# Background streams beside the first FFN of a macaron block: other places for transposes, routing and operand fetches

## The chip, the cores and the metric

The kernel runs on one core of a Trainium2 chip. The metric is the device time of one launch in microseconds, as the median of several runs. A core has five engines with an instruction queue each: TensorE (PE, matrix products into PSUM), VectorE (DVE), ScalarE (ACT), GpSimd (POOL) and SyncE (SP), which in this kernel issues the DMA transfers. Each engine takes its instructions in the order of the program, and engines wait for each other through semaphores.

## The reference, cut to what matters

The input x is (4, 1024, 128): 4096 tokens of width 128. A first mixture-of-experts FFN, an attention and a second FFN are added to it in turn:

```python
x = x + 0.5 * ffn(layernorm(x))
x = x + attn(layernorm(x))       # attn normalises its input again, adds it back
x = x + 0.5 * ffn(layernorm(x))

def ffn(x):                      # 8 experts, all of them computed for each token
    w = routing_weights(x, Wr, temperature)                # (.., 8)
    h = silu(einsum('btd,edi->beti', x, Wg)) * einsum('btd,edi->beti', x, Wu)
    return einsum('bte,betd->btd', w, einsum('beti,eid->betd', h, Wd))

def routing_weights(x, Wr, temperature):
    inh = sigmoid(x @ Wr / temperature)
    in_zone = (inh >= LOWER) & (inh <= UPPER)
    dist = abs(inh - 1 / e)
    w = exp(-dist / 0.1) * in_zone
    fb = exp(-dist / 0.3) * (one of its two largest)
    w = where(w.sum(-1) < 1e-8, fb / clip(fb.sum(-1), 1e-8), w)
    return w / clip(w.sum(-1), 1e-8)

def attn(x):                     # 16 heads of 64
    h = layernorm(x) * ln_scale + ln_bias
    c_q, c_kv = h @ w_down_q.T, h @ w_down_kv.T            # latents of width 64
    q, k = rope(c_q @ w_up_q.T), rope(c_kv @ w_up_k.T)
    v = c_kv @ w_up_v.T
    return softmax(q @ k.T / 8) @ v @ w_out.T + x
```

## The kernel before, in words

All 4096 tokens lie in SBUF as X, in eight blocks of 512 tokens. The kernel has three stages: the first FFN (about 10 to 231 us of the profile), the attention (about 235 to 1604 us) and the second FFN (to the end).

**The first FFN** (`ffn`) runs 64 iterations, n = 8 * block + expert. An iteration has six matmuls for the gate and the up product (L402, each product in three parts of a split into high and low halves), the silu on ACT (L404), the down product of the expert three iterations back (L373), the product of silu and up on DVE (L410), and the addition of a weighted expert output to X (`gather`): on DVE, or by a scaled copy on ACT (L385) and a sum on POOL (L386).

**Streams.** Between these, at four points of each iteration, `bg1` advances two generators that hold everything else. A generator does one step per `next` and pauses at each `yield`. A rate says how many steps a point is worth, with fractions saved up, so the place of each background instruction in each engine's queue follows from the counts of steps.

- Stream 0 (`RATE0` per point while n < 4, then `RATE1` = 2.4 steps an iteration) prepares the blocks in pairs (0,1), (2,3), (4,5), (6,7) with `ffn_pre`: statistics, the power on POOL, the norm (L225 on DVE for block 0, L227 on ACT for the others), four transposes on PE (L256) with copies on DVE (L258, L259), the router product (L269) with its reduction (L270), and for the pair together the routing (`route`). The number k is the step at which a part is done; the second block of a pair runs 5 steps behind the first. The first twelve steps of the first pair come before the FFN. The pairs (4,5) and (6,7) join the stream at n = 14.
- Stream 2 (`RATE2` = 2.3 steps an iteration until n = 46, `RATE3` = 1.4 after) holds the weights of the attention and from n = 16 `attn_first`: the attention's preparation of the first 1024 tokens (`attn_pre`: transposes L540, down products L546, transposes L561) and then nine rotations.

**Spare bank.** In the first FFN the transposes, router products and down products of the streams share one PSUM bank, `self.rest = [self.psS[3]]`, which `aux` hands out.

**Rotations** (`rope`). The 64 rotations make the rotated q and k, 512 tokens and two heads' worth at a time. One rotation fetches its operand C_l (two buffers, 512 KB) from DRAM ("fetch"), multiplies it (L595, "mm"), multiplies by cosines and sines on DVE (L583), adds on POOL (L602, L604), splits the result in halves (L609 on ACT, L613 on POOL) and stores both (hi_r and eo, "dhi" and "dlo"). `attn_first` starts a new rotation each 6 steps, and its table says how many steps before or after its "mm" each part is issued. Rotations 0 to 8 (`NROPE` = 9) belong to `attn_first`; what is left of them when the first FFN ends is issued there. Later ones follow the attention's loop.

**The seam.** At n = 46 `load(0)` brings q and k of the first heads in; from n = 49 on the attention's first pass for the row maxima (`passA`: L676 on PE, L677 on DVE) runs in the FFN already. After the FFN come `load(1)`, the rest of `attn_first`, and the fetch of rotation 9 (`rope(-1, {-2: "fetch"})`), all on SP's queue. Then the attention's loop: scores (L701), exponentials on ACT (L705), sums on POOL (L717), and values (L724).

**In `route`**, `more` is a further pause at four places. It was given by `self.slot >= 0`, and `self.slot` is negative until the attention begins:

```python
more = (None,) if self.slot >= 0 else ()
...
v.tensor_tensor(w, w, ge, ALU.mult)
yield from more
```

The last pair of the second FFN, (6,7), is prepared within it by `ffn_pre` too (`bg2`: one step an iteration from n = 17, two from n = 22).

Of the kernel before, what the change touches and what calls it, by code (L numbers as in the profile page):

```python
# [31 lines left out]
NROPE = 9  # L32
ACTS = (4, 6, 7)
WLAG, GS, GD = 4, 17, 22
RATE0, RATE1, RATE2, RATE3 = 1.55, 2.4, 2.3, 1.4


class Kernel:
# [191 lines left out]
    def ffn_pre(self, P, blks, xs, w_out, done=None, rows=None):  # L230
        nc = self.nc
        X = self.X
        n = len(blks)
        mv = P.tile([128, TPB, 2], F32, name="mvf")
        rstd = P.tile([128, TPB, 2], F32, name="rstdf")
        z = P.tile([128, TPB, E], F32, name="z")
        st = {}

        def stage(k, h, blk):
            t0 = 4 * blk  # L240
            hs = slice(4 * h, 4 * h + 4)
            src = [X[:, t0 + i, :] for i in range(4)]
            if k == 0:
                st["st", h] = self.small.tile([128, 4, 6], F32, name="st")
            if k in (0, 1):
                self.stats(st["st", h], src, mv[:, hs], rstd[:, hs], k)
            elif k == 3:
                self.power(rstd[:, hs])
            elif k in (5, 6):
                if k == 5:  # L250
                    st["y", h] = P.tile([128, 4, 128], F32, name="yf", tag="f0")
                self.norm(st["y", h], src, mv[:, hs], rstd[:, hs], k - 5, blk == 0 and done is None)
            elif k == 8:
                ps = self.aux()
                for i in range(4):
                    nc.tensor.transpose(ps[:, i * 128:(i + 1) * 128], st["y", h][:, i, :], self.ident)  # L256
                x2 = st["x", h] = xs(blk)
                nc.vector.tensor_copy(x2[:, 0, :], ps)  # L258
                nc.vector.tensor_tensor(x2[:, 1, :], ps, self.f(x2[:, 0, :]), ALU.subtract)  # L259
                self.ready.add(blk)  # L260
            elif k == 12:
                x2 = st["x", h]
                if done:
                    done(blk, x2)
                pz = self.aux()
                for i in range(4):
                    c = slice(i * 128, (i + 1) * 128)
                    for hl in range(2):
                        nc.tensor.matmul(pz[:, i * 16:(i + 1) * 16], x2[:, hl, c], self.wr[:, hl, :], start=hl == 0, stop=hl == 1)  # L269
                nc.vector.tensor_reduce(z[:, hs, :], pz[:, 0:64].rearrange("p (t k e) -> p t e k", t=4, k=2), AX.X, ALU.add)  # L270

        for k in range(14 + 5 * (n - 1)):
            yield any(k - 5 * h in (8, 12) for h in range(n))
            for h, blk in enumerate(blks):
                stage(k - 5 * h, h, blk)
        yield from self.route(P, 4 * n, z, w_out)
        if rows is not None:
            yield from self.weight_rows(P, rows)
        self.routed.update(blks)

    def route(self, P, T, z, w_out):

        nc = self.nc
        v, act, pool = nc.vector, nc.scalar.activation, nc.gpsimd
        sh, sh4 = [128, T, E], [128, T, E, E]
        bc = lambda t: t.unsqueeze(2).to_broadcast(sh)
        new = lambda name, shape, tag=None: P.tile([128, TPB] + shape, F32, name=name, tag=tag or name)[:, :T]


        inh, dist = new("inh", [E]), new("dist", [E])  # L290
        more = (None,) if self.slot >= 0 else ()
        yield
        act(inh, z[:, :T], AF.Tanh, scale=self.rtemp)
        act(inh, inh, AF.Identity, scale=0.5, bias=self.consts[:, 0:1])
        act(dist, inh, AF.Abs, bias=self.consts[:, 1:2])
        yield
        ex = P.tile([128, 2, TPB, E], F32, name="ex")[:, :, :T]
        dx = P.tile([128, 2, TPB, E], F32, name="dx")[:, :, :T]
        w, fb = ex[:, 0], ex[:, 1]
        act(w, dist, AF.Tanh, scale=-0.5 / 0.1)  # L300
        act(fb, dist, AF.Tanh, scale=-0.5 / 0.3)
        act(dx, ex, AF.Identity, scale=-1.0, bias=self.consts[:, 2:3])
        act(ex, ex, AF.Identity, bias=self.consts[:, 2:3])
        ge, le = new("ge", [E]), new("le", [E])
        pool.tensor_scalar(ge, inh, LOWER, None, ALU.is_ge)
        pool.tensor_scalar(le, inh, UPPER, None, ALU.is_le)
        pool.tensor_tensor(ge, ge, le, ALU.mult)
        yield
        v.reciprocal(dx, dx)
        yield  # L310
        pool.tensor_tensor(ex, ex, dx, ALU.mult)


        below = new("below", [E, E], "f1")
        pool.tensor_tensor(below, fb.unsqueeze(3).to_broadcast(sh4), self.tri.unsqueeze(1).to_broadcast(sh4), ALU.mult)
        yield
        v.tensor_tensor(w, w, ge, ALU.mult)
        yield from more
        s, ne, some = new("ws", []), new("ne", []), new("some", [])
        v.tensor_reduce(s, w, AX.X, ALU.add)  # L320
        v.tensor_scalar(ne, s, 1e-8, None, ALU.is_lt)
        v.tensor_scalar(some, s, 1e-8, None, ALU.is_ge)
        yield
        g = new("g", [E, E], "f0")
        v.tensor_tensor(g, fb.unsqueeze(2).to_broadcast(sh4), below, ALU.is_gt)
        yield
        v.tensor_reduce(le, g, AX.X, ALU.add)
        yield

        v.scalar_tensor_tensor(fb, le, 2.0, fb, ALU.is_lt, ALU.mult)  # L330
        yield from more
        r = new("fr", [])
        v.tensor_reduce(r, fb, AX.X, ALU.add)
        v.tensor_scalar(r, r, 1e-8, None, ALU.max)
        yield
        v.reciprocal(r, r)
        v.tensor_tensor(r, r, ne, ALU.mult)
        yield from more
        v.tensor_tensor(w, w, bc(some), ALU.mult)
        yield from more  # L340
        v.tensor_tensor(fb, fb, bc(r), ALU.mult)
        yield
        v.tensor_tensor(w, w, fb, ALU.add)
        v.tensor_reduce(s, w, AX.X, ALU.add)
        yield
        v.tensor_scalar(s, s, 1e-8, 2.0, ALU.max, ALU.mult)
        v.reciprocal(s, s)
        v.tensor_tensor(w_out, w, bc(s), ALU.mult)
# [270 lines left out]
    def attn_first(self):  # L619

        yield from self.attn_pre(0)
        steps = {-5: "fetch", 0: "mm e0 e1", 2: "e", 3: "o", 5: "hi0", 6: "hi1", 7: "dhi", 8: "lo", 10: "dlo"}
        for t in range(-5, 6 * (NROPE - 1) + 11):
            yield
            for n in range(NROPE):
                for stage in steps.get(t - 6 * n, "").split():
                    self.rope(n, stage)
# [146 lines left out]
    def run(self):  # L774
# [21 lines left out]
        with ExitStack() as ctx:  # L796
# [8 lines left out]
            wgen = self.ffn_weights1(fw, fp)  # L805
            first = pre(0, 0, 1)
            next(wgen)
            for n in range(12):
                next(first)
                if n in (5, 6):  # L810
                    next(wgen)
            self.router_weights()
            attn_weights = self.attn_weights()
# [47 lines left out]

        a, c, e = (NP - 3) % 3, (NP - 2) % 3, (NP - 1) % 3
        xs = [self.KT[c], self.QT[e], self.KT[e]]
        self.load(1)
        for _ in streams[2].pop() if streams[2] else ():
            pass
# [30 lines left out]
        def rope(g, table):  # L897
            for d, stages in table.items():
                n, r = divmod(g - d - 1, 4)
                if r == 0 and 0 <= n + NROPE < 16 * B and n >= 0:  # L900
                    for stage in stages.split():
                        self.rope(n + NROPE, stage)

        rope(-1, {-2: "fetch"})
        for g in range(NGRP + 1):
            s0 = 2 * g
            self.group, self.slot = g, s0
# [29 lines left out]
            if g < NGRP and g % 8 == 7:  # L937
                P = g // 8
# [91 lines left out]
```

## Time and profile before

| what | us |
|---|---|
| median of 3 runs (lowest, highest) | 1762.56 (1762.29, 1762.91) |
| the profiled execution's own time | 1766.25 |
| its span in the profile | 1764.5 |
| PE busy | 1681.8 |
| DVE, ACT, POOL busy | 1298.0, 912.9, 1463.0 |
| mean granted clock of PE | 0.986 |

The span runs from the first to the last instruction that the profile shows; the execution's own time has 1.75 us around it. Busy times are sums over an engine's instructions. A line of PE's timeline gives the start and the duration of a group of instructions, the engine, the line of the kernel, the output and the inputs, and in brackets the idle time before it and what ended that. A "granted clock" below 1 in a stretch means that PE ran below full speed there.

### The profile page before, as it was taken

To read this page: it belongs to the slowest core of one execution; us is meant where nothing else is said; L and a number is where in the kernel's file an instruction comes from. 1 tells how busy PE (TensorE), PEld (TensorE's weight loads), DVE (VectorE), ACT (ScalarE), POOL (GpSimd) and SP (SyncE) were. 2 spreads that over 40 slices of the span, in tenths; PEclk is the share of its full clock that TensorE was granted. 3 is DMA by queue.
4 is the path that set the end of the run, shared out by engine and by line. 5 is a ranking of instruction groups with operands and counts; after the bars stand their busy time and mean duration, and the time that the engine had idled before them with its cause. 6 is when DMAs were issued, how large, how long until landed. Compare 5 with 4: busy or idle time off the path is not lost.

```text
span 1764.5 us, 31143 instructions
## 1 busy us (share of the span) xinstructions
PE 1681.8 (95%) x11428; PEld 1009.1 (57%) x11428; DVE 1298.0 (74%) x2223; ACT 912.9 (52%) x1916; POOL 1463.0 (83%) x803
## 2 busy tenths in 40 slices
PE   6998989999999999999999999999999999999998
PEld 5777755555555555455555555555555555456777
DVE  6676757767877778877787777688677766835887
ACT  4666546455455444555544455444554544455554
POOL 4448779999899998999998899898999987676666
PEclk9999989999999999999999999999999999999999
DMA  6024445455445554445454544544455432024542
GB/s 201 1 72 160 151 132 144 133 151 149 111 126 140 142 135 121 121 133 144 133 133 121 145 130 124 145 120 121 121 145 142 121 99 62 1 86 114 138 127 101
DMA packets 241416, 215.99 MB, mean 122 GB/s; under 512 B 156784, under 2 KB 169712, under 8 KB 240624
## 3 DMA queue, kind: packets, MB, share of 16 engines
q1 hardware_dynamic: 241264, 214.01, 43.9%
q8 instruction: 89, 1.46, 0.4%
q14 instruction: 63, 0.52, 0.1%
HBM read 129.93 MB, written 84.02 MB: 121 GB/s over the span
## 4 chain that ended last, share of the span: by engine, by line
PE 76%; DVE 10%; ACT 6%; POOL 4%; issue 3%; DMA 1%; SPq 0%; ACTq 0%; POOLq 0%; DVEq 0%
PE psc L724 24%; PE ps_s L701 21%; PE ps_a L676 8%; ACT p L705 4%; PE ps_s L402 4%; PE ps_s L736 3%; PE ps_s L481 3%; DVE m L677 3%; PE psx L761 3%; POOL acc L717 2%; PE psx L436 2%; PE psx L595 2%; PE psc L373 1%; PE psc L481 1%; PE ps_s L546 1%
## 5 line engine op out<-in xcount | busy, mean ns | idle before, releaser
L677 DVE TENSOR_REDUCE m<-ps_a 128x2 f32<-128x1024 f32 x512 | 626.8, 1224 | 329.1 <-PE ps_a L676 328.1
L705 ACT ACTIVATE p<-ps_s 128x512 f32<-128x512 f32 x1024 | 530.3, 602 | 578.3 <-PE ps_s L701 549.5
L717 POOL TENSOR_TENSOR acc<-acc,p 128x1024 f32<-128x1024 f32 x320 | 762.1, 2382 | 60.0 <-ACT p L705 42.8
L724 PE MATMUL psc<-p,ckn 128*64 128x512 f32 x2048 | 498.9, 608 | 0.0
L701 PE MATMUL ps_s<-QT,KT 64*128 64x512 f32 x3072 | 446.4, 393 | 9.4 <-ACT dsb L738 6.1
L701 PEld LDWEIGHTS ps_s<-QT,KT 64*128 64x128 f32 x3072 | 290.8, 185 | 75.9 <-ACT dsb L738 9.2
L724 PEld LDWEIGHTS psc<-p,ckn 128*64 128x64 f32 x2048 | 124.7, 136 | 227.3 <-issue 216.0
L676 PE MATMUL ps_a<-KT,QT 64*128 64x512 f32 x1024 | 234.0, 450 | 18.8 <-DVE m L677 18.8
L676 PEld LDWEIGHTS ps_a<-KT,QT 64*128 64x128 f32 x1024 | 97.5, 184 | 239.9 <-DVE m L677 78.7
L717 POOL TENSOR_TENSOR acc<-p 128x1024 f32<-128x1024 f32 x64 | 151.7, 2371 | 67.4 <-ACT p L705 67.2
L701 PE MATMUL ps_s<-maxr,one_row 64*128 64x512 f32 x1024 | 206.3, 392 | 0.0
L613 POOL TENSOR_TENSOR eo<-eo,hi_r 128x1024 fp32r<-128x1024 f32 x64 | 154.0, 2407 | 19.3 <-ACT hi_r L609 19.3
L386 POOL TENSOR_TENSOR X<-X,dtmp 128x512 f32<-128x512 f32 x54 | 69.3, 1284 | 68.1 <-ACT dtmp L385 60.1
L701 PEld LDWEIGHTS ps_s<-maxr,one_row 64*128 64x128 f32 x1024 | 99.6, 185 | 21.8
L489 POOL TENSOR_TENSOR p<-eo,p 128x512 fp32r<-128x512 f32 x42 | 63.1, 1510 | 40.0 <-ACT p L488 34.9
L602 POOL TENSOR_TENSOR eo<-rt,rt 128x512 f32<-128x512 f32 x64 | 83.0, 1296 | 0.0
L766 DVE SCALAR_TENSOR_TENSOR X<-ps_s,rT,X 128x128 f32<-128x128 f32 x252 | 70.4, 341 | 16.7 <-PE ps_s L761 16.6
L604 POOL TENSOR_TENSOR eo<-rt,rt 128x512 f32<-128x512 f32 x64 | 82.4, 1287 | 0.0
L402 PE MATMUL ps_s<-xs,wg 128*128 128x512 f32 x192 | 66.3, 455 | 11.3 <-DVE p L410 10.1
L609 ACT CAST hi_r<-eo 128x512 fp32r<-128x512 f32 x128 | 74.0, 622 | 4.7 <-POOL eo L604 2.2
L766 DVE SCALAR_TENSOR_TENSOR X<-psx,rT,X 128x128 f32<-128x128 f32 x252 | 70.4, 342 | 0.0
L761 PEld LDWEIGHTS psx<-G,osb 64*128 64x128 f32 x504 | 65.5, 187 | 4.3
(190 smaller groups left out, 2197.7 us busy)
## 6 DMA issues: line engine op xcount, KB each, us to landing
C_l<-cs SPq DMA_DIRECT2D x64, 512.0 KB
QT<-qs SPq DMA_DIRECT2D x256, 128.0 KB
KT<-ks SPq DMA_DIRECT2D x256, 128.0 KB
qs<-hi_r SPq DMA_DIRECT2D x32, 512.0 KB
qs<-eo SPq DMA_DIRECT2D x32, 512.0 KB
ks<-hi_r SPq DMA_DIRECT2D x32, 512.0 KB
ks<-eo SPq DMA_DIRECT2D x32, 512.0 KB
wb<-wt SPq DMA_DIRECT2D x64, 256.0 KB
```

The lines of the kernel that those rows point to most:

```text
L402: nc.tensor.matmul(p, w[:, a, e, :], xs[:, c, :], start=k == 0, stop=k == 2)
L602: nc.gpsimd.tensor_tensor(w["eo"][:, 0, :], w[0, 0], w[1, 1], ALU.subtract)
L604: nc.gpsimd.tensor_tensor(w["eo"][:, 1, :], w[0, 1], w[1, 0], ALU.add)
L613: nc.gpsimd.tensor_tensor(w["eo"].bitcast(F32R), w["eo"], self.f(w["hi"]), ALU.subtract)
L676: nc.tensor.matmul(self.psA[:, hh, :], self.QT[P % 3][r, 0, q0:q0 + 128], self.KT[P % 3][r, 0, kk * 512:kk * 512 + 512], start=True, stop= ...
L677: nc.vector.tensor_reduce(self.m_of[U][:, :, qb, kk], self.psA, AX.X, ALU.max)
L701: nc.tensor.matmul(ps, w, x, start=k == 0, stop=k == 3)
L705: nc.scalar.activation(self.p_of[s][:, hh, :], ps, AF.Exp, scale=0.125)
L717: nc.gpsimd.tensor_tensor(acc, self.p_of[s - 1] if c == 1 else acc, self.p_of[s], ALU.add)
L724: nc.tensor.matmul(self.psC[64 * hh:64 * hh + 64, :], self.ckn[b % 2][:, c, :], self.p_of[s][:, hh, :], start=c == 0, stop=c == 7)
L761: nc.tensor.matmul(po[hh][:, i * 128:(i + 1) * 128], osb[r, i * 128:(i + 1) * 128], self.G[r, j, :], start=True, stop=True)
L766: nc.vector.scalar_tensor_tensor(x, po[hh][:, i * 128:(i + 1) * 128], rT[:, 4 * hh + i:4 * hh + i + 1], x, ALU.mult, ALU.add)
```

## The change

Four things are altered. In `ffn_pre` the transposes come at step 10 instead of 8 and the router product at step 14 instead of 12, for every pair; in the first FFN the second block of the first pair runs 9 steps behind the first instead of 5, and the first fourteen steps (twelve before) come ahead of the FFN. In `route` the four further pauses are also taken by the pairs (2,3), (4,5), (6,7) of the first FFN. The rotations of `attn_first` fetch their operand 8 steps before their product instead of 5, and `RATE2` is 2.4 instead of 2.3. The fetch of rotation 9 is issued directly after the first FFN, ahead of `load(1)`.

```diff
-RATE0, RATE1, RATE2, RATE3 = 1.55, 2.4, 2.3, 1.4
+RATE0, RATE1, RATE2, RATE3 = 1.55, 2.4, 2.4, 1.4
...
-            elif k == 8:
+            elif k == 10:
                 ps = self.aux()
...
-            elif k == 12:
+            elif k == 14:
                 x2 = st["x", h]
...
-        for k in range(14 + 5 * (n - 1)):
-            yield any(k - 5 * h in (8, 12) for h in range(n))
+        lag = 9 if blks[0] == 0 and done is None else 5
+        for k in range(16 + lag * (n - 1)):
+            yield any(k - lag * h in (10, 14) for h in range(n))
             for h, blk in enumerate(blks):
-                stage(k - 5 * h, h, blk)
-        yield from self.route(P, 4 * n, z, w_out)
+                stage(k - lag * h, h, blk)
+        yield from self.route(P, 4 * n, z, w_out, blks[0] > 0 or done is not None)
...
-    def route(self, P, T, z, w_out):
+    def route(self, P, T, z, w_out, late):
...
-        more = (None,) if self.slot >= 0 else ()
+        more = (None,) if late else ()
...
-        steps = {-5: "fetch", 0: "mm e0 e1", 2: "e", 3: "o", 5: "hi0", 6: "hi1", 7: "dhi", 8: "lo", 10: "dlo"}
-        for t in range(-5, 6 * (NROPE - 1) + 11):
+        steps = {-8: "fetch", 0: "mm e0 e1", 2: "e", 3: "o", 5: "hi0", 6: "hi1", 7: "dhi", 8: "lo", 10: "dlo"}
+        for t in range(-8, 6 * (NROPE - 1) + 11):
...
-            for n in range(12):
+            for n in range(14):
                 next(first)
-                if n in (5, 6):
+                if n in (5, 7):
                     next(wgen)
...
+        self.rope(NROPE, "fetch")
         self.load(1)
...
-        rope(-1, {-2: "fetch"})
```

## The prediction

> **What bounds the kernel now.** I read the page's totals and slices first, then what TensorE (PE) waited for in the first 240 us, then each such gap in the timeline with the queue it waited for, last the granted clock in stretches of 3.4 us.
>
> ```profile
> PE 1681.8 (95%) x11428; PEld 1009.1 (57%) x11428; DVE 1298.0 (74%) x2223; ACT 912.9 (52%) x1916; POOL 1463.0 (83%) x803
> PE   6998989999999999999999999999999999999998
> POOL 4448779999899998999998899898999987676666
> PEclk9999989999999999999999999999999999999999
> ```
>
> PE is the bound: 95% busy, its few dips in the first six slices (44 us each). The attention after them can give little: what is to be had is PE's gaps in the first FFN, up to 231 us, at the seam to the attention, and at the end. The waits name them (total, times, longest):
>
> ```profile
> PE ps_s L402 <- DVE p L410: 10.1, 7, 3.9
> PE ps_s L256 <- DVE yf L225: 7.0, 3, 6.6
> PE ps_s L402 <- ACT p L404: 4.1, 3, 2.6
> PE ps_s L256 <- ACT yf L227: 1.8, 3, 0.8
> PE psx L595 <- DMA C_l<-cs: 1.4, 1, 1.4
> ```
>
> Each kind has its place in PE's timeline:
>
> ```profile
> 75.64 0.71 PE L256 MATMUL ps_s<-ident,yf 128*128 128x128 f32 x2 [0.75 <-ACT yf L227]
> 104.95 1.65 PE L402 MATMUL ps_s<-xs,wu 128*128 128x512 f32 x3 [2.56 <-ACT p L404]
> 152.73 1.65 PE L402 MATMUL ps_s<-xs,wg 128*128 128x512 f32 x3 [3.92 <-DVE p L410]
> 187.15 0.49 PE L595 MATMUL psx<-C_l,wup 64*128 64x512 f32 x1 [1.42 <-DMA C_l<-cs]
> 245.74 0.79 PE L595 MATMUL psx<-C_l,wup 64*128 64x512 f32 x1 [3.46 <-DMA C_l<-cs]
> ```
>
> The 3.92 us at 152.73 go back to the last routing: DVE stood at L317 behind POOL, with L583 and L410 behind it. The 3.46 us at 245.74 go back to SP's queue, where the fetch of rotation 9 stood behind a store that waited for POOL:
>
> ```profile
> 148.44 0.23 DVE L317 TENSOR_TENSOR ex<-ex,ge 128x64 f32<-128x64 f32 x1 [3.55 <-POOL ex L311]
> ...
> 241.00 0.38 SPq L47 DMA_DIRECT2D qs<-eo  x1
> 241.43 0.47 SPq L47 DMA_DIRECT2D C_l<-cs  x1
> ```
>
> A gap also costs afterwards (window, length, PE busy, granted clock):
>
> ```profile
> 73.80:77.20 3.40, 1.77 (x12) 0.99 0.00 0
> 77.20:80.60 3.40, 3.40 (x9) 0.51 0.03 7
> 148.80:152.20 3.40, 0.01 (x1) 1.00 0.77 254
> 152.20:155.60 3.40, 2.87 (x7) 0.50 0.40 154
> ```
>
> The window after a half-empty one ran at half clock, and so gave away about 1.7 us. Eight such windows lie between 30 and 252 us.
>
> **Clock, row against rule.** The Trainium skill, "TensorE: Matmul & The Clock Gate", section "HAM oscillation — how this bites in real kernels", says: "The abstract rule is "no PE-idle gaps >~3.4µs."" By it only the gaps of 3.92 and 3.46 us carry a surcharge. The trace disagrees: 1.77 us of work in 3.40 (52%) was already followed by 0.51. By the rule the gaps of 75 to 110 us are worth their 6.9 us, by the trace 11.6. The measurement decides; but new short gaps then cost double too.
>
> **The change part by part**, against the profiled execution: span 1764.5, own time 1766.25 (1.75 around the span; 3.7 us or 0.2% above the median of 1762.56). I take the differences over to the median unchanged.
>
> 1. *Opening, n = 0 to 8* (first pair's second block 9 steps behind the first, all transposes and routers two steps later). Following the three queues by hand, the first L402 starts about 0.6 us earlier, that of n = 2 one later, n = 4 at 25.5 (26.76), n = 6 at 35.1 (34.46). DVE's norm (L225), copies and routing bound this stage, and none of it goes away. The first pair's routing still ends just ahead of the first gather. Value 0, bounds -1.5 and +1.5.
>
> 2. *Routing of blocks 2, 3* now at n = 13 to 18 with four more pauses. PE's gaps of 0.40 (62.19) and 0.44 (70.00) may go: -0.8 (-0.84 to 0).
>
> 3. *n = 18 to 30.* Before, blocks 4, 5 and the attention's first preparation both began at n = 16; now the blocks come some three iterations later. PE idled 0.75 + 0.82 + 1.28 + 0.27 + 0.39 + 2.56 + 0.87 = 6.9 us there, and three half-clock windows (77.2, 87.4, 104.3) cost 1.6 + 1.7 + 1.4 = 4.7: together 11.6. In the new order the two streams take turns on the single spare PSUM bank (L256, L269, L540, L546, L561). PE meets four places where a use follows another so closely that it waits for the reader of the first: I put 0.9 + 2.2 + 1.7 + 0.6 = 5.4 us on them, from the readers' rows (L258 0.68 and L259 0.69 on DVE, L562 0.42) and what is queued ahead of them (L410 0.63 to 0.68, L404). Nearest rows: waits of 0.62, 0.39 and 0.87 at such places before, and 98.39 to 102.84 (4.4 us) from an L546 to the L553 that read its result. Two half-clock windows with that: 3.3. So -11.6 + 8.7 = -2.9 (-8 to +4).
>
> 4. *n = 33 to 49*, routing of blocks 6, 7, now at n = 43 to 48. DVE's new order puts four L583 between L309 and L317, so POOL has some 3.8 us for L311, against the 3.55 us that DVE stood before. Gaps here: 0.50 + 3.92 + 0.23 + 1.03 = 5.7, half clock 1.4, together 7.1. But POOL was busy 40.49 us of the 46.70 from 128.60 to 175.30, and a rotation's sums (L602, L604, L613) are 1.29 + 1.28 + 2.38 = 4.97: when PE runs faster, POOL's ring of buffers is next. I credit a third: -2.5 (-5 to +2).
>
>    *Ports, row against rule.* "SBUF — State Buffer", section "Who interferes with whom", says that a DVE operation with two SBUF inputs and a GpSimd operation lock each other out for a whole instruction. That speaks against spreading a routing among a busy POOL: some 8 such operations, each held by up to one 1.28 us POOL operation, are 10 us of DVE. The trace shows less: L321 took 672 ns where its shortest took 171, and the last routing lost about 3.2 us in all that way. Its DVE was busy 32.37 of 46.70 us, so 3.2 us hide, 10 would not. I take the row.
>
> 5. *Earlier fetches* (8 steps ahead instead of 5). The C_l wait at 187.15 goes, -1.4; its two buffers are freed by the L595 two rotations back, so the fetch itself isn't held. Each fetch passes a store of the rotation before on SP's queue (0.36 to 0.47 us of issue each); the store is then as much later, and its readers (QT, KT loads) wait for the last one only. A routing is 2.6 us of POOL (L305, L306, L307, L311, L315: 0.38 + 0.37 + 0.32 + 0.45 + 1.11), and with the pauses it lies ahead of other sums: it may delay rotation 3's L613 and with it load(0) (issued 171.50 to 179.65) to the first L676 (182.32): +0.9. Net -0.5 (-1.4 to +2). Rotation 9's fetch is in part 6.
>
> 6. *The seam.* One ACT copy (L609, 0.62) fewer stands ahead of the table load: -0.6 (-0.6 to 0). The fetch of rotation 9 is issued behind the store at 223.5, ahead of load(1)'s 16 issues (227.63 to 236.4), instead of at 241.43; it lands long before use. The first L595 starts when PE is free, 245.74 - 3.46 = 242.28, and at full clock its six end at 243.25 (0.97; 1.58 now). L724 takes 1.94 as its next run does, not 3.68, and ends at 245.2; DVE's L677 ends at 244.46 and two L583 follow, to 245.8. The scores (L701) start at 245.8 to 245.9, not 251.37: -5.4 (-6.2 to -3.5; the bad end is a half clock that stays). load(1) is pushed back by one issue, 0.47 us: its tiles are wanted much later.
>
> 7. *Attention and second FFN.* The rotations' loop and the pauses there are as before. Rows of x2 and wt are written two steps later, iterations ahead of their readers: 0. The last pair's transposes come one iteration (2.4 us) after their norm: waits of 1.05 at 1660.59 and 1.05 at 1667.99 go, 0.5 may come back at L269 (0.45 now): -1.6 (-3.8 with the half clock of 1668; 0 if DVE is late again).
>
> Sum: 0 - 0.8 - 2.9 - 2.5 - 0.5 - 0.6 - 5.4 - 1.6 = -14.3: span 1750.2, own time of a profiled execution about 1752, median 1748.3.
>
> **Rivals.**
> - *Only the seam and the end gain.* Parts 2 to 5 cancel: new bank waits and POOL take back what was freed. For it: POOL's 40.49 of 46.70. 1762.56 - 0.6 - 5.4 - 1.6, and half a us lost: 1755.5.
> - *Everything goes.* The bank waits hide behind queued matmuls: parts 3 to 5 give -6 more: about 1742.
> - *Nothing measurable.* The attention takes up the seam (POOL was busy 19.84 of the 20 us from 280 to 300, so an earlier start may only wait there), and the first FFN gives nothing: 1761 to 1763.
> - *Slower: the single spare bank.* At the four places of part 3, PE's in-order queue holds all later matmuls until DVE and ACT, themselves behind L410 and L404, have read the bank. If each costs the 4.4 us of 98.39 to 102.84 and a half-clock window of 1.7, that is 24.4 us against the 11.6 removed: 12.8 lost. POOL then takes nothing more from parts 4 and 5 (0), and the other parts give 0.8 + 0.6 + 5.4 + 1.6 = 8.4: +4.4, 1767.0. It decides from a mean of about 4.2 us a place (4w + 6.8 - 11.6 - 8.4 = 3.5). Against it: three such places before cost 0.39 to 0.87.
> - *The change does not do what it says.* The built instruction order excludes most: the fetch stands ahead of load(1), L317 behind the four L583; the new `late` alters nothing in the attention, where these pauses were already on.
>
> **How the numbers follow.** About 0.2% (3.5 us) is what a measurement of this kernel can tell from no change. Chances: forecast (1744 to 1753) 0.46; seam and end alone, 1755.5, 0.20; all goes, 1742, 0.10; nothing measurable 0.12; slower 0.12. Faster (below 1759.0) is 0.76, same 0.12, slower (above 1766.1) 0.12. The range 1740 to 1760 takes in the first three, nearly whole, and the lower edge of the fourth: 0.8.
>
> **What would show it.** Right: no C_l wait at 187 or 246, the first attention L595 at about 235 us instead of 245.74, granted clock 1.00 through 241 to 252; no L317 wait of 3.55 and no 3.92 gap; L256 at the end without its two 1.05 waits. Wrong: new rows at L256, L269 or L540 waiting for L258, L259, L553 or L562 at 85 to 110 us that sum to more than 11; a rotation's L595 or L610 waiting for POOL; an L676 waiting for a QT or KT load near 182.

## The result, and the profile after

The changed kernel takes 1778.75 us (median of 5 runs, 1775.95 to 1779.09), the kernel before 1762.91 (1762.29 to 1763.15). The ratio is 1.0086, with a 95% interval from 1.0073 to 1.0098: it is slower by some 15.8 us, where 14.3 us less were forecast.

The two profiled executions differ by less, 1777.0 us of span against 1764.5, because the one shown of before was itself 3.3 us above the median of its kernel. To see where the time went I compare the starts of the same instruction in both traces: the silu of each iteration n of the first FFN, the exponentials of the attention (numbered from 0), the silus of the second FFN. (Lines from 272 on have moved down by one in the changed kernel: its L403 is L402 before.)

| stretch | forecast, us | traces, us |
|---|---|---|
| opening, n = 0 to 18 | -0.8 (parts 1, 2) | -0.1 |
| n = 18 to 30 | -2.9 (part 3) | +2.1 |
| n = 30 to 36 | in part 4 | -3.4 |
| n = 36 to 50 | -2.5 and -0.5 (parts 4, 5) | +12.7 |
| n = 50 to 63 | 0 | -1.6 |
| seam, to exponential 16 | -6.0 (part 6) | -6.9 |
| attention, to its end | 0 (part 7) | +7.2 |
| second FFN | -1.6 (part 7) | +2.9 |
| sum | -14.3 | +12.9 |

Differences of 1 to 2 us between two traces can be chance. Kernels 1, 11 and 14 of the experiments have the instructions of before up to n = 30; from n = 18 to 30 they took 46.6 to 47.4 us, the trace of before 48.7. Kernels 2, 7, 8, 12 and 13 have those of after there: 7, 12 and 13 took 49.2 us, 2, 8 and after itself 50.8. In both cases the longer traces have three windows at half clock in that stretch and the shorter ones have one.

The seam did what was forecast. Four stretches became longer instead: n = 18 to 30, n = 36 to 50, the attention and the second FFN. The totals already hint at the engine: PE and DVE are busy longer with the same instructions, DVE by 12.7 us (1298.0 before).

```profile
PE 1686.8 (95%) x11428; PEld 1013.4 (57%) x11428; DVE 1310.7 (74%) x2223; ACT 912.0 (51%) x1916; POOL 1463.1 (82%) x803
PE   7988989999999999999999999999999999999898
```

PE's waits up to 270 us (total, times, longest) have lost the two C_l rows and gained others:

```profile
PE ps_s L403 <- DVE p L411: 12.4, 9, 3.4
PE ps_s L403 <- ACT p L405: 5.5, 3, 2.8
PE ps_s L269 <- DVE rstd L222: 2.9, 1, 2.9
PE ps_s L541 <- DVE xs L259: 1.6, 1, 1.6
PE ps_s L269 <- DVE xs L259: 1.5, 1, 1.5
```

In PE's timeline they lie here. The first is one of the forecast bank waits: the profile names L222, an operation of 0.15 us, but right ahead of it DVE ran L554, which read the bank until 98.11. The other two are in the last routing, where the 3.92 us of before have gone and come back in pieces:

```profile
98.26 1.54 PE L269 MATMUL ps_s<-wr,xs 128*128 128x16 f32 x8 [2.89 <-DVE rstd L222]
...
176.61 1.25 PE L403 MATMUL ps_s<-xs,wg 128*128 128x512 f32 x3 [2.29 <-DVE p L411]
...
189.60 0.96 PE L403 MATMUL ps_s<-xs,wg 128*128 128x512 f32 x3 [3.20 <-DVE p L411]
```

Behind both stands DVE. Its timeline in the last routing, and POOL's at the same moments:

```profile
173.93 2.03 DVE L318 TENSOR_TENSOR ex<-ex,ge 128x64 f32<-128x64 f32 x1
...
183.66 2.06 DVE L338 TENSOR_TENSOR fr<-fr,ne 128x8 f32<-128x8 f32 x1
```

```profile
173.53 2.35 POOL L614 TENSOR_TENSOR eo<-eo,hi_r 128x1024 fp32r<-128x1024 f32 x1
...
183.31 2.39 POOL L614 TENSOR_TENSOR eo<-eo,hi_r 128x1024 fp32r<-128x1024 f32 x1
```

L318 took 0.23 us before, L338 0.17. Here each ends within 0.1 us of the POOL operation that was running when it began (175.96 beside 175.88, 185.72 beside 185.70). Such an operation I call held. Counted against each operation's shortest run in the same trace, the nineteen DVE operations of this routing lost 3.8 us before and 9.0 now (a count by buffer gives 8.2, and a rougher one 7.4; some expectations below use these). DVE's timeline has no idle time from 169 to 192 us, and L411, for which PE waits, stands in that queue.

The granted clock follows (window, length, PE busy, clock); each half-empty window is again followed by one at half clock:

```profile
173.70:177.10 3.40, 1.11 (x8) 1.00 0.09 34
177.10:180.50 3.40, 3.40 (x14) 0.50 1.04 278
187.20:190.60 3.40, 1.00 (x4) 1.00 0.95 266
190.60:194.00 3.40, 3.40 (x14) 0.52 0.97 364
```

But the last routing, which begins at 169.7 us, holds only half of what n = 36 to 50 lost. Ahead of it PE idles 1.64 + 0.56 + 2.80 = 5.0 us (at 143.62, 151.33 and 155.09), and two windows at half clock, 153.2 to 160.0, give away 3.4. From the routing's start to n = 50 it is 2.29 + 3.20 = 5.5 us of idle time and 3.4 of half clock, 8.9 in all, where before had 5.2 and 1.7, 6.9 in all, and nothing ahead of the routing. All three gaps go back to the norm of the last pair's blocks, which now lies among the rotations. Twice DVE stands at L222 (2.35 us ahead of 138.95, 2.29 ahead of 149.45), with L411 behind it. The second time L222 waits for POOL's power L216, which stands behind the rotations' L614 and L603, and is then held itself (1.22 us; 0.15 at its shortest). ACT's L227 waits for L222, and behind L227 in ACT's queue come 3.6 us of work and then the silu L405. (The profile of after puts L227's wait down to PE's L269, which ended 0.1 us later than L222; that of kernel 12, with the same wait, to L222.) The first line is DVE in after, the second DVE in before, the others are POOL, PE and the clock in after:

```profile
149.45 1.22 DVE L222 SCALAR_TENSOR_TENSOR rstdf<-mvf,rstdf 128x4 f32<-128x4 f32 x1 [2.29 <-POOL rstdf L216]
...
122.30 1.28 DVE L222 SCALAR_TENSOR_TENSOR rstdf<-mvf,rstdf 128x4 f32<-128x4 f32 x1 [0.49 <-POOL rstdf L216]
...
144.81 2.38 POOL L614 TENSOR_TENSOR eo<-eo,hi_r 128x1024 fp32r<-128x1024 f32 x1
147.14 1.29 POOL L603 TENSOR_TENSOR eo<-rt,rt 128x512 f32<-128x512 f32 x1
148.39 1.03 POOL L216 TENSOR_TENSOR rstdf<-rstdf,neghalf 128x4 f32<-128x4 f32 x1
...
155.09 1.65 PE L403 MATMUL ps_s<-xs,wu 128*128 128x512 f32 x3 [2.80 <-ACT p L405]
...
149.80:153.20 3.40, 1.93 (x13) 1.00 0.37 140
153.20:160.00 6.80, 4.91 (x18) 0.50 0.40 148
```

At the seam, SP issues the fetch of rotation 9 directly behind the store of the rotations and ahead of load(1). No C_l wait is left, and no half clock between 194 and 450 us:

```profile
234.80 0.36 SPq L47 DMA_DIRECT2D ks<-eo  x1
235.25 0.42 SPq L47 DMA_DIRECT2D C_l<-cs  x1
237.33 3.41 SPq L47 DMA_DIRECT2D QT<-qs  x4
```

In the attention the new gaps of PE are these two, of a kind with the routing's; DVE and POOL at the first of them come after:

```profile
1062.79 0.50 PE L677 MATMUL ps_a<-KT,QT 64*128 64x512 f32 x2 [2.06 <-DVE m L678]
1085.70 0.49 PE L677 MATMUL ps_a<-KT,QT 64*128 64x512 f32 x2 [2.06 <-DVE m L678]
```

```profile
1059.22 2.39 DVE L213 TENSOR_SCALAR rstdf<-mvf 128x4 f32<-128x4 f32 x1
1061.52 1.21 DVE L678 TENSOR_REDUCE m<-ps_a 128x2 f32<-128x1024 f32 x1
```

```profile
1056.74 7.27 POOL L718 TENSOR_TENSOR acc<-acc,p 128x1024 f32<-128x1024 f32 x3 [0.23 <-ACT p L706]
```

The POOL line holds three sums of 2.4 us each. L213, an addition on four numbers a partition, took 2.39 us beside the third of them instead of 0.17, and the maximum L678, on which PE's next product depends, came that much later.

At the end, the two waits of 1.05 us at L256 are gone and one of 3.99 us is there, at another line:

```profile
1681.40 0.97 PE L437 MATMUL psx<-p,QT 128*128 128x512 f32 x3 [3.99 <-ACT fo L450]
```

### The profile page after: what moved, and what is told of

Read it like the earlier page. It is cut to its first block, busy times and chain, and to the rows that moved or that the text cites. A ratio compares the mean times of both kernels' runs of the same rounds, so it can differ in the third digit from the quotient of the medians.

```text
span 1777.0 us, 31148 instructions
## 1 busy us (share of the span) xinstructions
PE 1686.8 (95%) x11428; PEld 1013.4 (57%) x11428; DVE 1310.7 (74%) x2223; ACT 912.0 (51%) x1916; POOL 1463.1 (82%) x803
## 4 chain that ended last, share of the span: by engine, by line
PE 69%; DVE 10%; POOL 6%; ACT 6%; issue 3%; SPq 1%; DMA 1%; POOLq 0%; DVEq 0%; ACTq 0%
PE psc L725 22%; PE ps_s L702 19%; PE ps_a L677 7%; ACT p L706 4%; POOL acc L718 3%; PE ps_s L403 3%; PE ps_s L737 3%; DVE m L678 3%; PE psx L762 2%; PE ps_s L482 2%; PE psx L596 1%; PE psx L437 1%; POOL p L490 1%; PE psc L374 1%; DVE rt L584 1%
## 5 line engine op out<-in xcount | busy, mean ns | idle before, releaser
L678 DVE TENSOR_REDUCE m<-ps_a 128x2 f32<-128x1024 f32 x512 | 626.5, 1224 | 325.1 <-PE ps_a L677 324.4
L614 POOL TENSOR_TENSOR eo<-eo,hi_r 128x1024 fp32r<-128x1024 f32 x64 | 153.4, 2398 | 21.7 <-ACT hi_r L610 21.7
L603 POOL TENSOR_TENSOR eo<-rt,rt 128x512 f32<-128x512 f32 x64 | 82.5, 1290 | 2.1 <-DVE rt L584 2.1
L403 PE MATMUL ps_s<-xs,wg 128*128 128x512 f32 x192 | 66.8, 459 | 13.4 <-DVE p L411 12.4
```

The costliest lines, as they stand in the source:

```text
L403: nc.tensor.matmul(p, w[:, a, e, :], xs[:, c, :], start=k == 0, stop=k == 2)
L603: nc.gpsimd.tensor_tensor(w["eo"][:, 0, :], w[0, 0], w[1, 1], ALU.subtract)
L614: nc.gpsimd.tensor_tensor(w["eo"].bitcast(F32R), w["eo"], self.f(w["hi"]), ALU.subtract)
L678: nc.vector.tensor_reduce(self.m_of[U][:, :, qb, kk], self.psA, AX.X, ALU.max)
```

## The experiments

Each of them alters the changed kernel ("after") or the kernel before; "kernel 1" is that of experiment 1, and so on. Their medians stand beside 1778.75 for after, measured once, and 1763.1 to 1763.8 for before, measured again beside each group of them. A "loss" is what DVE's operations of the last routing lose, counted as above.

**1. The seam alone.** Before, with

```diff
+        self.rope(NROPE, "fetch")
         self.load(1)
...
-        rope(-1, {-2: "fetch"})
```

> The kernel before with one edit alone: the fetch of rotation 9 directly after the first FFN, ahead of load(1). If the seam is worth what the prediction said, the first scores of the attention start 5 to 7 us earlier, no C_l wait is left at 246 us, and the time is 1757 (1755.5 to 1758). Rival, the attention's own limits (POOL, DVE) take it up: 1761 to 1763 with the same earlier first score.

1759.12 us, ratio 0.9979 (0.9970 to 0.9987). The seam, from the last silu of the first FFN to exponential 16, is 6.3 us shorter than before, where 6.0 were forecast; 4.0 show in the median, which lies 1.1 us above the range expected. The mechanism holds; the attention takes back 1.3 us of the gain in this trace.

**2. The later steps in the attention and the second FFN undone.** After, with

```diff
+        KT, KR = (10, 14) if done is None and rows is None else (8, 12)
...
-            elif k == 10:
+            elif k == KT:
...
-            elif k == 14:
+            elif k == KR:
```

> The changed kernel, with the transposes and the router product of the attention's and the second FFN's preparations back at steps 8 and 12; the first FFN and the seam stay changed. Theory: the two later steps shift DVE's and POOL's work beside the attention (5.7 us lost between 950 and 1235 us) and at the end (2.6 us): about 1770.5, and PE leaves the attention some 6 us earlier than in the changed kernel. Rival: those losses come of where in the clock's windows the gaps fall and not from the steps: 1777 to 1780.

1768.28 us: 10.5 us back. The traces show +1.8 instead of +7.2 over the attention and -1.4 instead of +2.9 over the second FFN. So the later steps cost two thirds of the loss in stages for which the forecast had a zero and a gain. L213 of these preparations shows it (minimum, median, maximum in ns; the first line after, the second this kernel):

```profile
L213 DVE TENSOR_SCALAR rstdf<-mvf x6: 169/1558/2389, 714.2 to 1413.3; 128x4 f32<-128x4 f32 x6
```

```profile
L213 DVE TENSOR_SCALAR rstdf<-mvf x6: 170/420/1893, 714.7 to 1407.9; 128x4 f32<-128x4 f32 x6
```

**3. No further pauses in the first FFN.** After, with

```diff
-        yield from self.route(P, 4 * n, z, w_out, blks[0] > 0 or done is not None)
+        yield from self.route(P, 4 * n, z, w_out, done is not None)
```

> The changed kernel without the four further pauses in the first FFN's routings. Theory that the pauses stretch the last routing (blocks 6, 7) into the iterations where its result is due and beside POOL's rotations, where DVE loses 7.4 us to operations that take longer: the first FFN ends 5 to 8 us earlier and the time is 1771 to 1774. Rival that the later steps alone do it (the routing starts at n = 43 either way): within 2 us of 1778.

1778.26 us, no difference: the first theory falls as it was put. The trace shows two effects that nearly cancel. Without pauses n = 36 is reached 4.7 us later than in after, and n = 36 to 50 then costs +8.3 instead of +12.7, with a loss of 6.0 instead of 9.0 us in the last routing.

**4. The first FFN's steps undone, pauses and fetches kept.** After, with steps 8 and 12, `lag` 5 and twelve steps ahead in the first FFN (the attention's at 10 and 14).

> The changed kernel with the first FFN's preparations as before (transposes at step 8, router product at 12, second block of the first pair 5 steps behind, twelve steps ahead of the FFN); pauses, fetches and RATE2 stay changed. Theory that the later steps cost: the last routing starts two iterations earlier, at n = 41, and no bank waits of L269 at 98 us: 1768 to 1771. Rival that the pauses are the cause: 1776 to 1779.

1773.21 us: 5.5 us back, short of the 8 to 11 expected. The first FFN ends 5.1 us earlier than in after. The loss is 7.5 us, and ahead of the last routing PE idles 1.5 us from n = 36 on, where it was 5.0. A wait of 2.90 us at L269 is there all the same (103.77), so the bank waits belong not to the later steps alone.

**5. and 6. Fetches alone, pauses alone.** Kernel 1 with the fetches at -8 and RATE2 = 2.4, and kernel 1 with the pauses.

> The kernel before with the early fetch of rotation 9, and with it the rotations' fetches 8 steps ahead and RATE2 = 2.4; steps and pauses as before. Theory that these fetches are harmless and only take the C_l wait of 1.4 us away: 1757 to 1759 (the fetch of rotation 9 alone gave 1759.1). Rival that the quicker rotations crowd POOL and DVE in the last routing and cost 3 us or more: 1762 to 1765.

> The kernel before with the early fetch of rotation 9 and the four further pauses in the first FFN's routings; steps, fetches and RATE2 as before. Theory, from the runs so far: the pauses help up to n = 36 (some 4 us) and stretch the last routing beside POOL (some 5 us lost): 1758 to 1761. Rival that they cost throughout: 1764 to 1767.

1763.54 and 1762.12 us against 1759.12: +4.4, the rival's case, and +3.0, between the two cases. Both lengthen the last routing's loss: 3.8 us in kernel 1, 5.7 and 8.4 here. Neither helps by itself. Neither has the 5.0 us of idle time ahead of the last routing either (0 and 0.7), so that comes of the alterations together.

**7. and 8. The held operations, from both sides.** After, once with four DVE operations of the last routing left out, once with POOL's L614 taken off POOL in the three rotations beside it:

```diff
-        v.tensor_tensor(w, w, ge, ALU.mult)
+        if full:
+            v.tensor_tensor(w, w, ge, ALU.mult)
...
+        elif stage == "lo" and n in (2, 3, 4):
+            for k in range(2):
+                nc.scalar.activation(w["eo"][:, k, :].bitcast(F32R), w["eo"][:, k, :], AF.Identity, scale=0.0)
```

> The changed kernel without four of DVE's operations in the last routing of the first FFN (L318, L331, L338, L340: the mask, the top-2 mask and two scalings of the routing weights of blocks 6 and 7 are left out). They are worth 0.8 us at their shortest and took 6.2 us. Theory that DVE's small operations are held by POOL's long ones and that this is what makes DVE late for L411: the first FFN ends 4 to 6 us earlier and the time is 1772 to 1775. Rival, POOL itself or the deadline of the last routing is the bound: less than 2 us earlier, 1777 to 1779.

> The changed kernel with POOL's subtraction L614 (2.4 us each) of rotations 2, 3 and 4 replaced by two ACT operations that write zeros (the low halves of those rotations are left out). POOL then has 7.2 us less beside the last routing, ACT 3 to 4 us more. Theory of the held operations: the time that DVE loses in that routing falls from 8.2 us to 4 to 5, and the first FFN ends 3 to 6 us earlier: 1773 to 1776. Rival that DVE loses the time to its own order and not to POOL: the loss stays at 8, and no more than 2 us of gain.

1773.03 us (1771.35 to 1775.37) and 1771.39 us (1770.47 to 1773.7): 5.7 and 7.4 us back, and the first FFN ends 5.5 and 4.5 us earlier in the traces. Part of that is chance: in kernel 13's trace, with the instructions of after in the whole first FFN, it ends 4.1 us earlier as well. The stretch from the last routing's start to n = 50 is clearer. There PE idled 5.5 us and half clock gave away 3.4 in after and in kernel 2 (the same instructions), 4.9 and 1.7 in kernel 13; it idled 2.9 us in kernel 7 and 2.5 in kernel 8, with no half clock. The loss is 4.4 us in kernel 8, 9.0 in after and 7.0 in kernel 13. Kernel 7 leaves POOL's work as it is, which speaks against POOL itself as the bound. In kernel 8 DVE's instructions are those of after, in the same order, and the same two operations are half as long or at their shortest:

```profile
175.51 0.92 DVE L318 TENSOR_TENSOR ex<-ex,ge 128x64 f32<-128x64 f32 x1
...
182.54 0.17 DVE L338 TENSOR_TENSOR fr<-fr,ne 128x8 f32<-128x8 f32 x1
```

**9. Pauses for blocks 2 to 5 alone; 10. and a quicker stream 0.** Kernel 1 with the pauses of the first two of the three routings, then also with `bg(0, (RATE1 if n < 20 else 2.8) / 4)`.

> The kernel before with the early fetch of rotation 9 and the four further pauses in the routings of blocks 2 to 5 alone, not in the last one of the first FFN. Theory that only the last routing is hurt by pauses: 1757 to 1760, the best so far or equal to 1759.1. Rival that the pauses of the first routings push the last one further into the rotations all the same: 1761 to 1763.

> The same with RATE1 = 2.8 instead of 2.4 from n = 20 on, which brings the last routing about two iterations forward, away from the rotations. Theory that it is the last routing's place beside POOL's rotations that counts: DVE loses under 4 us in it, 1755 to 1758. Rival that a faster stream 0 crowds the stage before it, with bank waits: 1760 to 1763.

1767.70 and 1761.67 us. The first is worse than either case: the pauses push the last routing from 141 to 158 us in the trace, beside the rotations, and its loss is 8.3 us. Brought forward to 146 us, its loss is 3.8 us, as the theory had it, and 6 us come back; but not below kernel 1, because n = 30 to 36 costs 2.3 us more. The routing is not all of it: from kernel 9 to kernel 10 n = 36 to 50 becomes 7.0 us shorter and n = 18 to 30, where kernel 9 is 8.1 us behind kernel 1, becomes 6.0 shorter, while n = 30 to 36 becomes 4.5 longer. For the loss, where the last routing lies counts for more than whether it has pauses itself: 8.3 us without them at 158 us, 8.4 with them at 154 (kernel 6), 3.8 without them at 146.

**11. and 12. Shorter operations on POOL.** L614 of the first nine rotations in two halves, once in kernel 1, once in after:

```diff
-            nc.gpsimd.tensor_tensor(w["eo"].bitcast(F32R), w["eo"], self.f(w["hi"]), ALU.subtract)
+            for k in range(2):
+                nc.gpsimd.tensor_tensor(w["eo"][:, k, :].bitcast(F32R), w["eo"][:, k, :], self.f(w["hi"][:, k, :]), ALU.subtract)
```

> The kernel before with the early fetch of rotation 9, and POOL's subtraction L613 of the first nine rotations in two halves (about 1.3 us each instead of one of 2.4). Theory that DVE's small operation is held until POOL's running operation ends: the loss in the last routing falls from 4.0 to about 3, 1757.5 to 1759.5. Rival that the added 0.2 us a rotation on POOL and the more frequent handing over cost more: 1760 to 1762.

> The changed kernel with the same split of the first nine rotations' subtraction (L614). Theory that the hold lasts as long as POOL's operation: no operation of the last routing is held for 1.9 us or more any longer (L318 and L338 were held 1.8 and 1.9), the loss of 9 us falls to about 7, the first FFN ends 1 to 3 us earlier: 1775.5 to 1778. Rival that DVE is held as often as there are operations on POOL: no less loss, 1778 to 1780.

1759.36 us (nothing gained over 1759.12; the loss stays at 4.0) and 1772.70 us, 6.1 us back in after. There POOL does the same work and DVE the same operations, and L318 and L338 are held less:

```profile
171.74 0.70 DVE L318 TENSOR_TENSOR ex<-ex,ge 128x64 f32<-128x64 f32 x1
...
179.32 0.96 DVE L338 TENSOR_TENSOR fr<-fr,ne 128x8 f32<-128x8 f32 x1
```

By themselves these two show little, since they are held less in kernel 13 too, where POOL's operations are whole, and L322 (0.42 in after) is held instead:

```profile
171.95 0.41 DVE L318 TENSOR_TENSOR ex<-ex,ge 128x64 f32<-128x64 f32 x1
...
173.12 1.52 DVE L322 TENSOR_SCALAR ne<-ws 128x8 f32<-128x8 f32 x1
...
180.32 1.09 DVE L338 TENSOR_TENSOR fr<-fr,ne 128x8 f32<-128x8 f32 x1
```

Over the whole routing, no operation of kernel 12 loses more than 1.1 us, less than one of POOL's pieces of 1.28 to 1.29; the most is 1.9 in after and 1.4 in kernel 13. The loss is 6.9 us, against 9.0 and 7.0, and PE idles 4.0 us in the routing with no half clock. So the holds do get shorter with POOL's pieces, but what that is worth is not settled. The 6.1 us are more than the 1 to 3 expected, and in the trace 1.6 of them come between n = 18 and 30, before the first split operation (143 us).

**13. and 14. The held operation in the attention.** L213 on POOL instead of DVE once the attention runs, in after and in kernel 11:

```diff
-            nc.vector.tensor_scalar(rstd[:, :, 1], mv[:, :, 1], EPS, None, ALU.add)
+            (nc.gpsimd if self.slot >= 0 else nc.vector).tensor_scalar(rstd[:, :, 1], mv[:, :, 1], EPS, None, ALU.add)
```

> The changed kernel with one small operation moved from DVE to POOL in the attention: the addition of epsilon to the variances (L213), which comes just ahead of POOL's power anyway. In the changed kernel it was held by POOL up to 2.39 us, twice right ahead of a gap of PE of 2.06 us (1062.79 and 1085.70). Theory of the held operation: both gaps go and PE is 3 to 5 us earlier after 1110 us: 1773.5 to 1776. Rival that the next operation (L222) is held in its place or that POOL's added operation delays the exponentials' sums: 1777 to 1780.

> The kernel before with the early fetch of rotation 9, the subtraction of the first nine rotations in two halves, and the same move of L213 to POOL in the attention. There L213 was held 1.9 us at most and little of PE's idle time hung on it: 1757.5 to 1759.5, no worse than the 1759.1 and 1759.4 without the move. If POOL's added operation costs: 1760 to 1762.

1760.94 us (1758.52 to 1767.1): 17.8 us less than after, four times what was expected, and level with before (0.9984 to 1.0004). In the traces 4.1 of the 17.8 come of the first FFN, where the instructions are the same, and so are chance. And 1751.72 us (1751.07 to 1756.41), ratio 0.9937 (0.9925 to 0.9949): the fastest kernel of this study. On POOL the operation takes 0.22 to 0.27 us:

```profile
L213 POOL TENSOR_SCALAR rstdf<-mvf x6: 218/229/245, 710.7 to 1399.9; 128x4 f32<-128x4 f32 x6
```

Both gaps of 2.06 us are gone, and from 1000 to 1235 us this kernel keeps step with before, where after fell back 6 us. I had underrated it because I looked only where after differs from before. L213 is held in both. In before too, and not at most 1.9 us as I had expected of kernel 14, it took 2.37 us at 447 and at 665 us, each time ahead of a gap of 2.04 us:

```profile
447.01 2.37 DVE L213 TENSOR_SCALAR rstd<-mv 128x4 f32<-128x4 f32 x1
449.30 1.21 DVE L677 TENSOR_REDUCE m<-ps_a 128x2 f32<-128x1024 f32 x1
...
450.56 0.50 PE L676 MATMUL ps_a<-KT,QT 64*128 64x512 f32 x2 [2.04 <-DVE m L677]
```

In kernel 14 some 7 us of its gain over kernel 11 come by 760 us, from such places. Over the attention L213 loses 15.7 us in after, 11.5 in kernel 2 and 11.2 in before. From exponential 16 to the first silu of the second FFN the attention takes 1351.9 us in after and 1346.5 in kernel 2; with L213 on POOL it takes 1336.9 with the later steps (kernel 13) and 1336.2 with the earlier ones (kernel 14). So the later steps cost the attention 5.4 us through L213 and 0.7 without it. The rival, L222 held in its place, is small: L222 loses 22.8 us in kernel 13, 21.4 in after. That is more than L213 lost, and no run tries to move it.

## Why the prediction was wrong, point by point

- *Part 6, the seam: right.* -6.0 forecast, -6.9 in the trace, -6.3 in kernel 1 alone.
- *Parts 1 and 2:* -0.1 instead of -0.8, which is within what a trace varies by.
- *Part 5:* the C_l wait went, and no L676 waited for load(0). But the fetches and RATE2 together cost 4.4 us (kernel 5 against 1) where -0.5 was forecast. The step had counted SP's queue and not that the rotations' operations on POOL then lie elsewhere beside the last routing. In the traces kernel 5 falls 5.1 us behind kernel 1 from n = 36 to 50; it also falls 3.5 behind from n = 18 to 30, whose cause was not looked for.
- *Part 4, the last routing: this is the step that failed in the first FFN,* with two errors. The routing's gaps and half clock were to fall from 7.1 us by 2.5; they came to 8.9. The mechanism named for the gain was right: L317's wait of 3.55 us and the gap of 3.92 us went. The hold was weighed too, and put at the 3.2 us "in all" of the row before (3.8 by the count used here), because "Its DVE was busy 32.37 of 46.70 us, so 3.2 us hide, 10 would not. I take the row." By the rule of the Trainium skill ("SBUF — State Buffer", section "Who interferes with whom") the later of the two "fully blocks" until the other is done; the estimate worked out from it with POOL's 1.28 us was up to 10 us, and the run gave 9.0. That the two come so close is partly luck: not eight holds of 1.28 us came but two of 1.8 and 1.9 and several shorter ones. The row held for its own place and not for the new one, six iterations later and more (n = 43 to 49 instead of 37 to 41 in the traces) and stretched by pauses, where DVE has no idle time left. Kernels 7 and 8 show the hold as the cause; kernel 12 agrees. The second error is a term that is missing: the last pair's norm, too, now waits for POOL among the rotations, and with it 8.4 us are lost ahead of the routing, where nothing was lost before. This is read from the trace; no run alters it alone. (The rotation's sums in this part, 1.29 + 1.28 + 2.38, make 4.95 and not 4.97, which changes nothing.)
- *Part 3, bank waits: right in size, wrong in the balance.* 5.4 us of waits at the shared bank were forecast, and 0.68 + 2.89 + 1.60 + 0.58 = 5.8 came between 91 and 111 us, with 5 us of half clock instead of 3.3. What was missed: the removed waits did not all go away. PE now waited for ACT's silu, 1.61 us at 77.01 and 1.13 at 82.96. Net +2.1 instead of -2.9, where a trace varies by 1 to 2 us. The rival "slower" had named this bank and needed 4.2 us a place, where 1.4 came; the direction was right, but the bank is not what made the kernel slower.
- *Part 7, the attention: this step failed too, put at 0 and measured at +7.2.* The part costed the rows of x2 and wt that the two later steps write, and said that loop and pauses were as before. But `ffn_pre` is also what prepares blocks in the attention: two more steps there move all later background steps against POOL's 2.4 us sums, and some of these steps are DVE operations that can be held. The 10.5 us of kernel 2 (with the second FFN) show that the steps are the cause; the 5.4 us that become 0.7 in kernels 13 and 14 show that they cost this by way of L213.
- *Part 7, the end: -1.6 against +2.9.* The waits at L256 had only been the place where PE met a late ACT: it stood behind DVE's L222 for the norm of the next block (2.16 us idle ahead of L227 at 1678.23, as 2.17 before). With the transposes later, PE ran on and met the same lateness at the copy of its output bank, L450, which sits behind that norm in ACT's queue, as 3.99 us.
- *The clock:* the price read from the trace stands, with the proviso of the last section. 1.11 and 1.00 us of work in 3.40 were followed by half clock, with no gap above 3.3 us there, against the rule "no PE-idle gaps >~3.4µs" of the Trainium skill ("TensorE: Matmul & The Clock Gate", section "HAM oscillation — how this bites in real kernels").
- *Left open:* the parts taken singly do not add up. Pauses +3.0, fetches +4.4, the first FFN's steps 5.5 and the others' 10.5 make 23.4 over kernel 1, and after is 19.6 over it. The stretches interact, since each moves the last routing. Of the 3.3 us by which the profiled execution of before was slow, 1.4 to 2.1 lie between n = 18 and 30, by the traces of kernels 1, 11 and 14; where the rest lies was not found.

## What to carry to other kernels

A move of background work is priced at its new place: list every small DVE operation that moves, ask which long POOL operation runs there, and ask what stands in POOL's queue ahead of a result that DVE and ACT wait for. Count every stage that shares the function, not only the one the change is about. And when a short DVE operation shows two durations, as L213 does with 0.17 and 2.39 us, moving it off DVE or splitting POOL's long operations may be worth more than any order of streams: here 8 us from one line.

## What the runs showed of the hardware

- Held on DVE were operations with two inputs in SBUF, and `tensor_scalar` on SBUF alone: in the trace of after L213 took from 0.17 to 2.39 us, L323 from 0.16 to 2.39, L222 from 0.15 to 2.35, L331 from 0.21 to 2.27. Never held were reductions (L678, 1.20 to 1.23 in 512 instances), reciprocals (L749, 0.19 to 0.20) and operations with an input in PSUM (L411 at most 0.69, L584 at most 0.69). No hold in this trace is longer than 2.3 us, one POOL operation of 2.4.
- Whether a gap costs half a clock window as well depends on where it falls. In each of the two traces, before and after, all stretches at half clock begin on one fixed grid of 3.41 us. The same gap of 2.04 us stood at 450.56 us before, where it left PE 2.0 us of work in the window of the grid that it fell in most, and at 453.38 after, where it left 1.4; only the second was followed by a window at 0.50, and 1.6 us of difference between the two traces come of that. From 40 us on to 15 us before the end, all 15 full-clock windows of the grid with less than 1.69 us of PE's work were followed by half clock in these two traces, and none with more than 2.2.
